# A transformer block in fp32: which engine subtracts the softmax maximum beside the feed-forward layers

## The chip, the core and the metric

The kernel runs on one core of one Trainium2 chip. A core has five engines with instruction queues of their own: TensorE (PE in the profile; its weight loads are listed as PEld), VectorE (DVE), ScalarE (ACT), GpSimd (POOL), and SyncE (SP), which here only issues transfers. Each engine works through its queue in order. The metric is the device time of one execution in microseconds (us). Before the change three runs gave 3252.26, 3256.43 and 3268.8 us; their median, 3256.43 us, is the time before.

## The reference

One pre-norm transformer block on x of shape (2, 1024, 1024): attention with 32 heads of size 32 over 1024 tokens, then a gated feed-forward layer of width 2752, all in fp32.

```python
def attn(x, qkvw, qkvb, ow, ob):
    qkv = x @ qkvw + qkvb                     # 1024 -> 3 * 1024
    ...
    scores = jnp.einsum('bhqd,bhkd->bhqk', q, k) * scale
    probs = jax.nn.softmax(scores, axis=-1)
    ctx = jnp.einsum('bhqk,bhkd->bhqd', probs, v)
    ...
    return ctx @ ow + ob

def ffn(x, W_gate, W_up, W_down):
    up = xt @ W_up.T
    gate = jax.nn.silu(xt @ W_gate.T)
    return (gate * up @ W_down.T).reshape(out_shape)

x = x + attn(_layernorm(x), ...)
x = x + ffn(_layernorm(x), ...)
```

## The kernel before

**Phases and units.** Attention is cut into four phases (two batches, two blocks of 512 queries each), and each phase into 16 units of two heads. A unit works through eight key tiles `kt` of 128 keys. For each tile it holds scores of 128 keys by 1024 (two heads by 512 queries), keys on the partitions. Unit `n` belongs to phase `n // 16`.

**What a unit does** (class `Unit`):

- `scores` (matmul L510) writes two score tiles into PSUM (tag `s`, two buffers). `largest` (L524, VectorE) folds each into a running maximum `top`, reading the scores from PSUM; `keep` (L529, ScalarE) copies them to `p` in SBUF. Both have to be done before the PSUM buffer is free for the next scores.
- `maximum` takes the maximum over keys on VectorE (L549, L550, L567, L568), stores its negative to DRAM (L573) and loads it again, broadcast to all partitions, into `m` (L576).
- `less_maximum` (L580 to L590) adds `m` to `p` in place, 128x1024 elements with both inputs in SBUF (L583). The engine is chosen in L582.
- `exponential` (L593, ScalarE) follows, again in place.
- `add` (L606) adds neighbouring tiles of `p`, three additions for each group of four tiles, a running sum: tile 1 gets tile 0, tile 2 gets tile 1, tile 3 gets tile 2. In phase 0 VectorE does all of them; in phases 1 to 3 tiles 3 and 7 go to VectorE and tiles 1, 2, 5 and 6 to GpSimd. `differences` (L599, GpSimd) prepares the values so that these sums may stand in for the tiles themselves.
- `values` (matmuls L622) multiplies with the values and with ones, into PSUM (tag `acc`, one buffer), and `finish` copies the result out.

**What runs beside it.** While phase 0 runs, TensorE does the projections to q, k and v (L371, L433) for both batches, and GpSimd adds up weights for later (L1189). While phases 1, 2 and 3 run, TensorE does the rest of the block for the 512 tokens of the phase before: the output projection (L785, evicted by VectorE at L797), the second normalization with its transposes (L259), and the feed-forward layer. Beside the tail, the rest for the last 512 tokens, there is no attention.

**The feed-forward layer** uses seven products instead of eight for two-by-two blocks. `product` makes gate and up (matmuls L927): each product of four matmuls goes to one PSUM bank and is evicted by VectorE (L941 to L954) or ScalarE (L939); `silu` (L955) and the product of gate and up (L957, VectorE, both inputs in SBUF) follow. After every four chunks of 128 hidden columns a down projection follows, `down_steps`: `down7` (matmuls L1076), whose accumulators VectorE adds to the residual `x` (L1089, L1091), one or two such operations for two matmuls; `sums_h` forms the sums of hidden columns on VectorE (L1045 to L1051, both inputs in SBUF). `down` (L1003, L1014) is the plain form for the last part, and `hold` and `release` (L1026, L1027 on GpSimd; L1032, L1034 on VectorE) change the residual into the form that the seven products need and back. All these accumulators share three PSUM banks (tag `lin`, `lps`). GpSimd also multiplies the attention output by the reciprocal sums (L733) and adds the output bias to `x` (L777).

**What sets the order.** No scheduler reorders instructions. `Emitter` walks through lists of steps with a virtual clock: `run` interleaves the paced attention steps (one beat for each key tile) with the steps of the filling work, and `later(delay, fn)` puts off a step until the virtual clock has passed the delay. The order in which steps come out is the order in each engine's queue, and the tile framework adds the waits. `less_maximum` is a step of its own in `attention_steps`, eleven beats after the scores of the same tile; it puts off the exponential by 3.5 us of the virtual clock and the addition by 8.1 to 10 us. The choice of an engine does not enter the virtual clock.

Of the kernel before, what the change touches and what calls it, by code (L numbers as in the profile page):

```python
# [130 lines left out]
def preln_block_kernel(  # L131
# [14 lines left out]
    nc = tc.nc  # L146
# [318 lines left out]
    class Unit:  # L465
# [113 lines left out]

        def less_maximum(self, kt):  # L580
            p = self.p[kt]
            eng = nc.vector if self.phase == 0 and kt % 4 == 3 else nc.gpsimd  # L582
            eng.tensor_tensor(p, p, self.m, ALU.add)  # L583
            em.later(3500.0, lambda: self.exponential(kt))
            if kt % SUMS > 0:

                vec = self.phase == 0 or kt % RUN == RUN - 1
                delay = 8100.0 if self.phase == 0 else 10000.0 if vec else 9500.0
                eng = nc.vector if vec else nc.gpsimd
                em.later(delay, lambda: self.add(kt, eng))  # L590
# [767 lines left out]
```

## Time and profile before

| what | before |
|---|---|
| median of three runs | 3256.43 us |
| the profiled execution, its span | 3272.8 us |
| mean granted TensorE clock | 0.986 |
| L583 on GpSimd | 480 instructions, 1197.0 us, mean 2.508 us |
| L583 on VectorE | 32 instructions, all between 165.1 and 788.2 us |
| L606 on GpSimd | 192 instructions, 466.8 us, mean 2.431 us |
| L606 on VectorE | 192 instructions, 328.1 us, mean 1.709 us |
| L524 on VectorE (top from top) | 384 instructions, 469.1 us, mean 1.222 us |
| L1089 on VectorE | 360 instructions, 235.7 us, mean 0.680 us |
| ScalarE's wait at L593 for GpSimd's L583 | 325.6 us |
| GpSimd's wait at L606 for ScalarE's L593 | 346.8 us |

The profile is of one execution, so sums of its durations are to be compared with its own span. The span runs from the first to the last instruction. A group's line gives its busy time, the mean duration of one instruction, and the idle time of its engine just before it with what ended that. A line of the timeline gives start, duration, engine, source line and operation, then in brackets the idle time before it and what ended it; `x3` means that three neighbours were merged. Phase 0 takes the first 890 us or so, phases 1 to 3 lie between 890 and 2790 us, and the tail follows. A wait counted for an engine costs time only where the engine is the one that the end waits for.

### The profile page before, as it was taken

Reading aid. Unit: us, or ns where it says so; the run is one execution under the profiler, and the core shown is the slowest. Engines: PE = TensorE matmul, PEld = TensorE weight load, DVE = VectorE, ACT = ScalarE, POOL = GpSimd, SP = SyncE. Lnnn points to the kernel's source line nnn. Section 1 sums busy time; section 2 is a strip of 40 time slices with the busy share of each in tenths; the row PEclk is TensorE's granted clock in tenths of the full one; section 3 lists DMA queues with packets and bytes.
Section 4 is the critical chain, followed back from the end, with each engine's and each line's share of the span. In section 5 each row is a group of like instructions: output and inputs, shape, how many; then the busy total and the mean of one; then the engine's idle time right before and its main releaser. Section 6 shows DMA issues by size and latency. Waiting matters only on the chain.

```text
span 3272.8 us, 42759 instructions
## 1 busy us (share of the span) xinstructions
PE 3166.3 (97%) x15488; PEld 1785.6 (55%) x15488; DVE 2012.2 (61%) x2733; ACT 1446.8 (44%) x1585; POOL 2039.6 (62%) x1079
## 2 busy tenths in 40 slices
PE   8999999999999999998899999988999999999999
PEld 4444434444346666563376655633756567477775
DVE  2266766776356777766577777666777774344334
ACT  2244554544456555563665555635655554010000
POOL 0267766777788777667887777777877777200000
PEclk9999999999999999998999999989999999999999
DMA  4566756655434554555344444562445445544452
GB/s 154 167 182 203 228 181 197 195 186 164 145 109 139 155 150 150 149 153 180 98 146 150 148 146 146 151 184 92 140 146 151 149 140 149 168 152 154 153 153 96
DMA packets 337825, 507.24 MB, mean 155 GB/s; under 512 B 105424, under 2 KB 122064, under 8 KB 337616
## 3 DMA queue, kind: packets, MB, share of 16 engines
q1 hardware_dynamic: 281424, 405.91, 40.4%
q10 hardware_dynamic: 56192, 98.60, 9.8%
q8 instruction: 124, 2.03, 0.3%
q14 instruction: 85, 0.70, 0.1%
HBM read 429.14 MB, written 75.24 MB: 154 GB/s over the span
## 4 chain that ended last, share of the span: by engine, by line
PE 79%; DVE 8%; POOL 4%; DMA 3%; issue 3%; ACT 2%; SPq 1%; ACTq 0%; POOLq 0%; DVEq 0%
PE p L927 30%; PE pq L371 13%; PE pd L1076 9%; PE acc L622 8%; PE s L510 7%; PE pvv L433 6%; PE po L785 4%; POOL p L583 2%; DVE x L1089 2%; DVE top L524 1%; DVE p L606 1%; PE pd L1003 1%; PE pg L971 1%; POOL p L606 1%; DVE h L957 1%
## 5 line engine op out<-in xcount | busy, mean ns | idle before, releaser
L583 POOL TENSOR_TENSOR p<-p,m 128x1024 f32<-128x1024 f32 x480 | 1197.0, 2508 | 15.9 <-DMA m<-d 15.9
L529 ACT COPY p<-s 128x1024 f32<-128x1024 f32 x512 | 516.3, 1012 | 730.0 <-DVE top L524 553.6
L593 ACT ACTIVATE p<-p 128x1024 f32<-128x1024 f32 x512 | 529.6, 1056 | 379.2 <-POOL p L583 325.6
L606 POOL TENSOR_TENSOR p<-p,p 128x1024 f32<-128x1024 f32 x192 | 466.8, 2431 | 352.5 <-ACT p L593 346.8
L524 DVE TENSOR_TENSOR top<-s,top 128x1024 f32<-128x1024 f32 x384 | 469.1, 1222 | 289.0 <-PE s L510 272.0
L927 PE MATMUL p<-sum,m 128*128 128x256 f32 x2688 | 610.4, 382 | 1.4 <-ACT gate L939 0.9
L927 PEld LDWEIGHTS p<-sum,m 128*128 128x128 f32 x2688 | 505.2, 190 | 101.1 <-issue 29.3
L927 PE MATMUL p<-xn2T,m 128*128 128x256 f32 x2016 | 469.5, 384 | 0.3 <-ACT xn2T L267 0.2
L371 PE MATMUL pq<-xnT,wqk 128*128 128x512 f32 x1024 | 457.4, 599 | 0.0
L1076 PE MATMUL pd<-wp,h 128*128 128x512 f32 x960 | 432.6, 598 | 15.2 <-DVE x L1089 15.0
L927 PEld LDWEIGHTS p<-xn2T,m 128*128 128x128 f32 x2016 | 382.6, 192 | 87.0 <-issue 29.8
L606 DVE TENSOR_TENSOR p<-p,p 128x1024 f32<-128x1024 f32 x192 | 328.1, 1709 | 105.2 <-ACT p L593 70.4
L371 PEld LDWEIGHTS pq<-xnT,wqk 128*128 128x128 f32 x1024 | 190.2, 190 | 249.4 <-issue 247.7
L510 PE MATMUL s<-q,k 32*128 32x512 f32 x2048 | 312.6, 650 | 12.0 <-ACT p L529 12.0
L1076 PEld LDWEIGHTS pd<-wp,h 128*128 128x128 f32 x960 | 177.7, 190 | 251.1 <-issue 197.0
L1189 POOL TENSOR_TENSOR ws<-raw 128x512 f32<-128x512 f32 x62 | 89.8, 1448 | 298.3 <-DMA raw<-in_w_gu 190.7
L1089 DVE TENSOR_TENSOR x<-pd,x 128x512 f32<-128x512 f32 x360 | 235.7, 680 | 52.6 <-PE pd L1076 52.2
L622 PE MATMUL acc<-p,vals 128*32 128x256 f32 x4096 | 254.6, 389 | 11.3 <-DVE p L606 11.3
L433 PE MATMUL pvv<-wv,xnT 128*128 128x512 f32 x512 | 231.1, 601 | 0.2 <-DVE vv L445 0.2
L785 PE MATMUL po<-wo,ctx 128*128 128x512 f32 x512 | 229.7, 601 | 0.8 <-DMA wo<-in_w_o 0.8
L622 PEld LDWEIGHTS acc<-p,vals 128*32 128x32 f32 x4096 | 121.4, 111 | 181.6 <-issue 97.7
L990 POOL MEMSET h<- 64x512 f32 x4 | 2.1, 524 | 298.9 <-PE pd L1076 298.9
(94 smaller groups left out, 2520.2 us busy)
## 6 DMA issues: line engine op xcount, KB each, us to landing
m<-dws SPq DMA_DIRECT2D x336, 256.0 KB
m<-in_w_gu SPq DMA_DIRECT2D x252, 256.0 KB
wp<-ddn SPq DMA_DIRECT2D x160, 256.0 KB
m<-d SPq DMA_DIRECT2D x64, 512.0 KB
wp<-in_w_dn SPq DMA_DIRECT2D x120, 256.0 KB
raw<-in_w_gu ACTq DMA_DIRECT2D x84, 256.0 KB
dws<-ws ACTq DMA_DIRECT2D x84, 256.0 KB
x<-in_x SPq DMA_DIRECT2D x32, 512.0 KB
```

The lines of the kernel that those rows point to most:

```text
L371: nc.tensor.matmul(ps, wqk[b, g, w, hk][:, k, :], xnT[b, s][:, kc, :], start=(kc == 0), stop=(kc == KC - 1),)
L433: nc.tensor.matmul(st["ps"], xnT[b, t // TB][:, kc, (t % TB) * P : (t % TB + 1) * P], st["w"][kc], start=(kc == 0), stop=(kc == KC - 1),)
L510: nc.tensor.matmul(ps[a][:, h * NH : (h + 1) * NH], self.k[rows, i * P : (i + 1) * P], self.q[rows, :], start=True, stop=True,)
L524: nc.vector.tensor_tensor(self.top, s, self.p[0] if kt == 1 else self.top, ALU.max)
L529: nc.scalar.copy(self.p[kt], s)
L583: eng.tensor_tensor(p, p, self.m, ALU.add)
L593: nc.scalar.activation(self.p[kt], self.p[kt], AF.Exp, scale=SCALE)
L606: eng.tensor_tensor(self.p[kt], self.p[kt], self.p[kt - 1], ALU.add)
L622: nc.tensor.matmul(self.acc[j * HD : (j + 1) * HD, c : c + NQ], w(h), self.p[kt][:, q0 : q0 + NQ], start=start, stop=stop, skip_group_chec ...
L785: nc.tensor.matmul(st["ps"], ctxT[b, blk][:, g, t * P : (t + 1) * P], st["w"][hf, g], start=(g == 0), stop=(g == G - 1),)
L927: nc.tensor.matmul(ps, mats[c, n][:, kc, :], rhs, start=(kc == 0), stop=(kc == hk - 1),)
L1076: nc.tensor.matmul(st["pd"], lefts[n](pi)[:, j, t * P : (t + 1) * P], st["wp", pi, n, j], start=(j == 0), stop=(j == PART // 2 - 1),)
```

## The change

One line in `less_maximum`. In phase 0 the choice stays as it was: tiles 3 and 7 of each unit on VectorE, the others on GpSimd. In phases 1 to 3, beside the output projections and the feed-forward layers, GpSimd did all eight; after the change VectorE does tiles 1, 3, 5 and 7. The operands, the place of the step in the emitted order and the delays of what follows stay the same.

```diff
         def less_maximum(self, kt):
             p = self.p[kt]
-            eng = nc.vector if self.phase == 0 and kt % 4 == 3 else nc.gpsimd
+            mine = kt % 4 == 3 if self.phase == 0 else kt % 2 == 1
+            eng = nc.vector if mine else nc.gpsimd
             eng.tensor_tensor(p, p, self.m, ALU.add)
             em.later(3500.0, lambda: self.exponential(kt))
             if kt % SUMS > 0:
```

## The prediction

> **What bounds the kernel now.** I read the page's totals first, then the chain that ended last, then the stages.
>
> ```profile
> span 3272.8 us, 42759 instructions
> ...
> PE 3166.3 (97%) x15488; PEld 1785.6 (55%) x15488; DVE 2012.2 (61%) x2733; ACT 1446.8 (44%) x1585; POOL 2039.6 (62%) x1079
> ...
> PE 79%; DVE 8%; POOL 4%; DMA 3%; issue 3%; ACT 2%; SPq 1%; ACTq 0%; POOLq 0%; DVEq 0%
> ```
>
> TensorE is the bound: only 107 us of the span are without a matmul. The totals of VectorE (61%) and GpSimd (62%) look alike, but they are averages. So I cut the span into stages with the view of busy time by stretch. Its columns are the stretch, its length, then PE, PEld, DVE, ACT and POOL busy us (instructions), granted clock, DMA share, GB/s. The first line is all that the change touches; the next three are two of the fourteen stretches in which a down projection (L1076) runs beside attention, and the sum of all fourteen.
>
> ```profile
> 890.00:2790.00 1900.00, 1823.10 (x10077) 1093.12 (x10076) 1301.49 (x1816) 1026.53 (x1096) 1471.30 (x746) 0.98 0.48 145
> ...
> 1164.00:1197.00 33.00, 31.29 (x126) 13.19 (x125) 30.45 (x40) 15.22 (x16) 23.19 (x11) 1.00 0.47 140
> ...
> 2376.00:2410.00 34.00, 32.39 (x128) 13.41 (x127) 32.10 (x41) 15.11 (x16) 23.71 (x10) 1.00 0.43 132
> ...
> sum 468.00, PE 449.90 PEld 187.15 DVE 421.67 ACT 213.44 POOL 328.78; mean PE 32.14 PEld 13.37 DVE 30.12 ACT 15.25 POOL 23.48
> ```
>
> In 890 to 2790 us, 77 us are without a matmul. In the fourteen stretches VectorE is busy 421.7 of 468 us (90%), GpSimd 70%: VectorE is nearly full there, not GpSimd. The timeline shows both kinds of stall, one of each below.
>
> ```profile
> 1186.47 2.54 DVE L524 TENSOR_TENSOR top<-s,top 128x1024 f32<-128x1024 f32 x2
> 1188.92 1.28 DVE L1089 TENSOR_TENSOR x<-pd,x 128x512 f32<-128x512 f32 x2
> ...
> 1190.26 1.98 PE L1076 MATMUL pd<-wp,h 128*128 128x512 f32 x4 [1.71 <-DVE x L1089]
> ...
> 1515.78 2.34 POOL L583 TENSOR_TENSOR p<-p,m 128x1024 f32<-128x1024 f32 x1
> 1518.07 2.35 POOL L606 TENSOR_TENSOR p<-p,p 128x1024 f32<-128x1024 f32 x1
> ...
> 1520.45 3.35 DVE L606 TENSOR_TENSOR p<-p,p 128x1024 f32<-128x1024 f32 x1 [8.89 <-POOL p L606]
> ...
> 1523.72 1.87 DVE L1014 TENSOR_TENSOR x<-pd,x 128x512 f32<-128x512 f32 x3
> ...
> 1524.46 1.22 PE L1003 MATMUL pd<-wd,h 128*128 128x512 f32 x1 [8.48 <-DVE x L1014]
> ```
>
> First kind: two maxima stand ahead of the accumulator's eviction in VectorE's queue, and TensorE waits 1.71 us for a PSUM bank. Second kind: VectorE waits 8.89 us for GpSimd's addition, TensorE 8.48 us behind it. I went through every TensorE gap over 0.25 us between 890 and 2790 us: eleven go back to GpSimd (1.25, 0.28, 3.20, 8.48, 0.48, 0.38, 2.69, 1.66, 11.70, 1.31, 8.44: 40 us), all where one block's down projection or output projection hands over to the next; some 18 us are short waits for VectorE in the down projections; four, together 15.6 us, stand ahead of the transposes of the second normalization.
>
> **What a subtraction costs on VectorE.** The change removes 192 instructions from GpSimd (4 of 8 key tiles, 16 units, 3 phases) and puts 192 into VectorE's queue; the instruction lists of both programs show just this, and no other step, DMA or queue entry moves. GpSimd loses 192 x 2.46 us (its mean at L583 from 890 us on) = 472 us. What VectorE pays depends on what GpSimd does meanwhile:
>
> ```profile
> 0.00:890.00 890.00, 60.23 (x32) 300.09 (x113) 0.99 0.58 182
> ...
> 1177.47 1.21 DVE L606 TENSOR_TENSOR p<-p,p 128x1024 f32<-128x1024 f32 x1
> ...
> 2239.51 12.18 DVE L606 TENSOR_TENSOR p<-p,p 128x1024 f32<-128x1024 f32 x1
> ```
>
> The first line is L583 alone in the first stage, where VectorE already does a quarter of the subtractions: 60.23 / 32 = 1.88 us each. The second is an operation of the same shape with GpSimd idle: 1.21 us. The 3.35 us above and the 12.18 us here began while GpSimd ran. Of the 92 VectorE additions from 890 us on, the 55 that met no GpSimd instruction took 1.21 us on average, the 31 that began during one 2.68 us. The maxima at L524 (one input from PSUM) take 1.22 us either way. So with both inputs in SBUF a VectorE operation is held while GpSimd works. Bounds per subtraction: 1.21 and 2.68 us. I take 1.88: the same line, and GpSimd's share there (548 of 890 us, 62%) is near what it falls to (below).
>
> The Trainium skill, "SBUF — State Buffer", section "Who interferes with whom", speaks against this change: a VectorE instruction with two SBUF inputs contends with a GpSimd instruction that reads SBUF, and the one that issues second is blocked until the first finishes. The 3.35 us agrees, but the 12.18 us does not: five GpSimd tensor operations passed during it. By the rule a single loss is at most 2.36 + 1.21 us, and 192 such would be 685 us of VectorE time; by the row there is no such cap.
>
> **The sum by stage.** *Down projections.* 86 subtractions start on GpSimd in the fourteen stretches; half, 43, move: 43 x 1.88 = 81 us. Against that, the four feed-forward sums of each stretch (L1045 to L1051, means 1.41, 1.17, 1.49 and 1.70 us against 0.68 alone) lose 3.06 us per stretch to GpSimd, 43 us in all; GpSimd's time there falls by 43 x 2.46 = 106 of 329 us, a third, so 14 us come back. VectorE then needs 421.7 + 81 - 14 = 489 us. The fullest stretch now reaches 97% (31.06 of 32 us); of 468 us that is 454. What does not fit, 35 us, falls on TensorE, because the moved operation stands straight behind the maxima and ahead of the next eviction, as in the first stall; what is late next is the matmul that needs the bank. Bounds: at 1.21 us with all 43 us returned nothing is pushed out and TensorE's 18 idle us could go: -18; at 2.68 us and nothing returned, 421.7 + 115 - 454 = 83.
>
> *The rest.* The other 141 moved operations (367 / 2 - 43) add 265 us to 880 of 1432 us: VectorE goes from 61% to 80%. In the gate and up products the cover is two further PSUM banks, each four matmuls of 0.215 us, 1.7 us together: 1.21 hides, 2.68 is 1.0 over. Without that cover, a third held of some 100 such operations costs 33 us. A pair of maxima (2.55 us) passes there without a stall now, so I take 5. The four transposes stand behind VectorE steps: one operation each, 4 x 1.88 = 7. Together 12, bounds 0 and 40.
>
> *Gain.* In the 8.48 and 11.70 us stalls one of the subtractions ahead of GpSimd's addition goes: 2 x 2.34; in the 2.69 us one the same, 2.3. The 8.44 us stall is the 12.18 us operation, held by an unbroken GpSimd run with L583 three times in it; with a hole in that run it goes: 8.4. The 1.66 and 3.20 us stalls I leave: VectorE is full there too. That is 15.4 us. The granted clock in these places is 0.81, 0.77 and 0.87 (1485 to 1530, 2160 to 2190, 2230 to 2270 us): 31.9 x 0.19 + 18.3 x 0.23 + 31.6 x 0.13 = 14 us, of which 15.4 / 28.6, some 7, come back. Gain 22; bounds 0 and 40 + 14 = 54. A second wait for the broadcast maximum costs nothing: GpSimd's even tile waits for the same transfer one beat earlier.
>
> Sum: 35 + 12 - 22 = +25 us on the profiled 3272.8, that is 3298. The profiled execution lies 16 us (0.5%) over the runs' median of 3256.43, so the forecast for the median is **3281 us**.
>
> **Rivals.** *GpSimd's relief decides (faster).* For it: all long stalls go back to GpSimd, which is 77% busy from 890 us on (1471 of 1900) and would fall to 54%. Against it: VectorE is fuller in the down projections. If most operations fall into the holes that they make, at 1.21 us: 43 x 1.21 - 14 = 38 against 32 us of room, +6, nothing elsewhere, and all 40 us of stalls gone: -34, 3222 us. It decides from a mean price below 1.30 us, where 43p - 14 - 32 + 12 equals 22.
> *Hidden anyway.* Small stalls on both sides cancel; for it: TensorE's queue keeps its order and 97%. 3256 us.
> *Starvation (slower still).* One of 92 additions was held for 12.18 us and stopped TensorE for 8.44 us at a clock of 0.87 (4 us more). At that rate 192 operations bring two: +25, 3306 us. Against it: GpSimd's runs get shorter. It matters from two events on.
> *That it doesn't do what it says* is out by the instruction lists.
>
> **How the numbers follow.** Forecast (slower, by VectorE in the down projections) 0.48, starvation 0.07, relief 0.27, hidden 0.18. A measurement of this kernel can tell about 0.5%, 16 us, from no change. So slower 0.55, within 0.18, faster 0.27. All bounds together give -72 to +123 us (3184 to 3379); eight in ten I put between 3220 and 3335, which holds the relief's 3222 and starvation's 3306. The likeliest case's own range is 3262 to 3312.
>
> **What would show it.** After: VectorE near 2350 us busy and GpSimd near 1570; L583 on VectorE 224 times at about 1.9 us; the fourteen stretches longer by 2 to 3 us each, with VectorE at 95% and more, and L1076 waiting for L1089 some 50 us instead of 18; the handover stalls of 8 to 12 us shorter, with a higher clock. I am wrong if the down projections keep their length (relief), or if gate and up products begin to wait for VectorE by tens of us (then it is slower than I say).

## The result and the profile after

The change makes the kernel slightly slower: 3275.68 us (median of 13 runs, 3269.82 to 3280.12) against 3257.06 us (13 runs, 3252.26 to 3275.14), a ratio of 1.004 with a 95% interval of 1.0027 to 1.0054. A second measurement gave 1.0031 (1.0015 to 1.0046). The ratios stand for +13 and +10 us (the medians of the two measurements lie 19 and 9 us apart). The forecast was 3281 us; its direction held, and its size, +25 us, is about twice what the ratios show.

The page of the profiled execution after: span, engine totals, and the chain that ended last.

```profile
span 3270.6 us, 42718 instructions
...
PE 3161.7 (97%) x15488; PEld 1777.3 (54%) x15488; DVE 2242.6 (69%) x2925; ACT 1447.0 (44%) x1585; POOL 1655.0 (51%) x887
...
PE 73%; DVE 18%; ACT 3%; DMA 3%; issue 2%; POOL 1%; SPq 0%; ACTq 0%; DVEq 0%; POOLq 0%
```

GpSimd's share of the chain falls from 4% to 1%, VectorE's rises from 8% to 18%. The bound has not moved from TensorE (97%); what TensorE waits for has. The groups of the changed line, L584 now, on both engines (busy us, mean ns):

```profile
L584 POOL TENSOR_TENSOR p<-p,m 128x1024 f32<-128x1024 f32 x288 | 750.5, 2611 | 20.6 <-DMA m<-d 20.5
...
L584 DVE TENSOR_TENSOR p<-p,m 128x1024 f32<-128x1024 f32 x224 | 404.1, 1804 | 0.0
```

192 subtractions moved, at 1.79 us each from 890 us on. VectorE's total rose by 230 us, though its subtractions rose by 344 (404.1 - 60.2). Some 84 us came off operations that GpSimd had held before: 32 us at the product of gate and up (from 1.51 to 1.00 us each for the 63 from 890 to 2790 us), 29 at the additions (328.1 to 299.1), 15 at the feed-forward sums and 8 at the operations on the residual with two SBUF inputs. The rest, some 29 us, is mostly that neighbouring instructions overlap a little in the record, so that their durations add up to more than the engine's busy time. GpSimd's own subtractions got longer, from 2.46 to 2.62 us: the hold goes both ways.

The timeline at the two places whose lines from before stand in the prediction. First a down projection:

```profile
1180.87 2.54 DVE L524 TENSOR_TENSOR top<-s,top 128x1024 f32<-128x1024 f32 x2
...
1183.33 1.22 DVE L584 TENSOR_TENSOR p<-p,m 128x1024 f32<-128x1024 f32 x1
...
1184.46 1.28 DVE L1090 TENSOR_TENSOR x<-pd,x 128x512 f32<-128x512 f32 x2
...
1185.79 1.98 PE L1077 MATMUL pd<-wp,h 128*128 128x512 f32 x4 [2.55 <-DVE x L1090]
```

The subtraction stands between the maxima and the eviction, and TensorE's wait has grown from 1.71 to 2.55 us. Then the handover from one block to the next:

```profile
1498.09 1.92 DVE L584 TENSOR_TENSOR p<-p,m 128x1024 f32<-128x1024 f32 x1
...
1510.85 2.34 POOL L584 TENSOR_TENSOR p<-p,m 128x1024 f32<-128x1024 f32 x1
...
1513.15 2.35 POOL L607 TENSOR_TENSOR p<-p,p 128x1024 f32<-128x1024 f32 x1
...
1515.53 3.36 DVE L607 TENSOR_TENSOR p<-p,p 128x1024 f32<-128x1024 f32 x1 [4.35 <-POOL p L607]
...
1519.54 2.08 PE L1004 MATMUL pd<-wd,h 128*128 128x512 f32 x2 [6.33 <-DVE x L1015]
```

Before, GpSimd did one more subtraction here, that of tile 7 of the unit, ahead of the lines that stand in the prediction:

```profile
1511.99 2.35 POOL L583 TENSOR_TENSOR p<-p,m 128x1024 f32<-128x1024 f32 x1
```

Now VectorE does that one, at 1498.09, so one subtraction (at 1510.85) instead of two stands directly ahead of GpSimd's addition, and TensorE's wait fell from 8.48 to 6.33 us. Waits of TensorE for VectorE from 890 to 2790 us (us in total, times, longest), first before, then after:

```profile
PE pd L1003 <- DVE x L1014: 20.2, 2, 11.7
PE pd L1076 <- DVE x L1089: 17.9, 26, 1.7
...
PE acc L622 <- DVE p L606: 11.3, 3, 8.4
```
```profile
PE pd L1077 <- DVE x L1090: 36.0, 39, 3.4
PE pd L1004 <- DVE x L1015: 16.1, 3, 9.5
...
PE acc L623 <- DVE p L607: 1.0, 1, 1.0
```

To see where the time went, I took lengths from each trace, from TensorE's own instructions: the four *handovers* (the first from the first output projection matmul, the others from a block's last matmul of L1076, each to the first gate product), the fourteen *down projections* beside attention (each from its first to its last matmul of L1076), and the *products*, the fifteen stretches that lead up to a down projection.

| profiled execution | handovers, each and sum, us | 14 down projections, us | products, us |
|---|---|---|---|
| before | 82.9, 121.2, 130.4, 75.3: 409.8 | 458.7 | 1081.0 |
| before, again | 83.3, 124.1, 127.9, 75.4: 410.7 | 458.1 | 1079.8 |
| before, a third time | 83.3, 127.1, 121.4, 72.4: 404.2 | 458.2 | 1080.0 |
| after | 76.7, 111.8, 115.4, 72.1: 376.0 | 483.3 | 1089.0 |
| after, again | 81.2, 113.4, 115.6, 72.2: 382.4 | 482.8 | 1088.2 |

On average: down projections +24.7 us, products +8.3, handovers -29. Of the last, 19 us are waits of TensorE (its idle time in the handovers fell from 45 to 26 us), and 10 us are shorter matmuls; the granted clock there rose from 0.94 to 0.97 on average. By place the sum is +4; the ratios say +10 to +13. Part of the difference may be chance in which executions were profiled: the three spans of before, 3266 to 3273 us, lie at or above the medians of before, 3257 to 3266 us. It was not followed further.

### The profile page after: what moved, and what is told of

Read it like the earlier page. It is cut to its first block, busy times and chain, and to the rows that moved or that the text cites. A ratio compares the mean times of both kernels' runs of the same rounds, so it can differ in the third digit from the quotient of the medians.

```text
span 3270.6 us, 42718 instructions
## 1 busy us (share of the span) xinstructions
PE 3161.7 (97%) x15488; PEld 1777.3 (54%) x15488; DVE 2242.6 (69%) x2925; ACT 1447.0 (44%) x1585; POOL 1655.0 (51%) x887
## 4 chain that ended last, share of the span: by engine, by line
PE 73%; DVE 18%; ACT 3%; DMA 3%; issue 2%; POOL 1%; SPq 0%; ACTq 0%; DVEq 0%; POOLq 0%
PE p L928 28%; PE pq L371 13%; PE s L510 7%; PE pd L1077 6%; PE acc L623 6%; PE pvv L433 6%; PE po L786 5%; DVE top L524 4%; DVE p L584 3%; DVE x L1090 3%; DVE p L607 1%; PE pd L1004 1%; DVE part L550 1%; ACT p L529 1%; PE pg L972 1%
## 5 line engine op out<-in xcount | busy, mean ns | idle before, releaser
L607 POOL TENSOR_TENSOR p<-p,p 128x1024 f32<-128x1024 f32 x192 | 498.3, 2595 | 693.5 <-ACT p L594 684.6
L584 POOL TENSOR_TENSOR p<-p,m 128x1024 f32<-128x1024 f32 x288 | 750.5, 2611 | 20.6 <-DMA m<-d 20.5
L1077 PE MATMUL pd<-wp,h 128*128 128x512 f32 x960 | 438.5, 602 | 32.8 <-DVE x L1090 32.3
L584 DVE TENSOR_TENSOR p<-p,m 128x1024 f32<-128x1024 f32 x224 | 404.1, 1804 | 0.0
L607 DVE TENSOR_TENSOR p<-p,p 128x1024 f32<-128x1024 f32 x192 | 299.1, 1558 | 91.4 <-ACT p L594 67.1
L1077 PEld LDWEIGHTS pd<-wp,h 128*128 128x128 f32 x960 | 176.3, 190 | 275.3 <-issue 187.8
L510 PE MATMUL s<-q,k 32*128 32x512 f32 x2048 | 304.6, 646 | 7.9 <-ACT p L529 7.9
L623 PE MATMUL acc<-p,vals 128*32 128x256 f32 x4096 | 254.7, 390 | 1.2 <-DVE p L607 1.0
L1190 POOL TENSOR_TENSOR ws<-raw 128x512 f32<-128x512 f32 x62 | 99.5, 1605 | 306.7 <-DMA raw<-in_w_gu 186.9
L623 PEld LDWEIGHTS acc<-p,vals 128*32 128x32 f32 x4096 | 121.5, 111 | 170.1 <-issue 96.3
```

The source lines that it names most:

```text
L510: nc.tensor.matmul(ps[a][:, h * NH : (h + 1) * NH], self.k[rows, i * P : (i + 1) * P], self.q[rows, :], start=True, stop=True,)
L607: eng.tensor_tensor(self.p[kt], self.p[kt], self.p[kt - 1], ALU.add)
L623: nc.tensor.matmul(self.acc[j * HD : (j + 1) * HD, c : c + NQ], w(h), self.p[kt][:, q0 : q0 + NQ], start=start, stop=stop, skip_group_chec ...
L1077: nc.tensor.matmul(st["pd"], lefts[n](pi)[:, j, t * P : (t + 1) * P], st["wp", pi, n, j], start=(j == 0), stop=(j == PART // 2 - 1),)
```

## Experiments

Ratios are to runs of the kernel before on the same chip, with 95% intervals.

**The kernel before, twice more** (no edit).

> The kernel before, profiled once more. If the 12.18 us addition and the handover stalls belong to the kernel, they come again at the same places and the span is near 3273 us; if they are chance, this span is some 10 us shorter and they sit elsewhere.

> The same a third time, for the spread of the handovers between executions of one kernel: the same lengths within 1 us if they are fixed, 5 us and more apart if they depend on how the engines happen to fall against each other.

Spans 3271.9 and 3266.3 us. The down projections repeat within 0.6 us, the handovers do not (the third: 130.4, 127.9, 121.4). What differs is the long hold of VectorE. The group of L606 on VectorE (minimum, median, maximum in ns), the second profile:

```profile
L606 DVE TENSOR_TENSOR p<-p,p x92: 1202/1216/12183, 903.5 to 2773.8; 128x1024 f32<-128x1024 f32 x92
```

and the timeline of the third:

```profile
1584.78 9.88 DVE L606 TENSOR_TENSOR p<-p,p 128x1024 f32<-128x1024 f32 x1
```
```profile
1583.86 4.71 POOL L583 TENSOR_TENSOR p<-p,m 128x1024 f32<-128x1024 f32 x2
1588.49 2.38 POOL L606 TENSOR_TENSOR p<-p,p 128x1024 f32<-128x1024 f32 x1
1590.79 2.37 POOL L583 TENSOR_TENSOR p<-p,m 128x1024 f32<-128x1024 f32 x1
1593.09 2.42 POOL L599 TENSOR_TENSOR vals<-vals 128x128 f32<-128x128 f32 x3
```

Each of the three profiles has a hold of 10 to 12 us, in a varying handover (one has two, 9.89 and 12.18), always in an unbroken GpSimd run. Neither profile after has one over 3.42 us. So the lost time there comes with this kernel each time, and its place varies.

**Only in the handovers, and only in the down projections.** The emitter carries the name of the place whose matmuls were emitted last; the choice asks for it (for the second kernel, for "down").

```diff
+        self.place = "handover"          # Emitter
...
         def product(c, n, kc):
+            em.place = "products"
...
         def down7(pi, n, t, j):
+            em.place = "down"
...
         def down(pi, hf, t, ci):         # and project() of oproj_steps
+            em.place = "handover"
...
-            mine = kt % 4 == 3 if self.phase == 0 else kt % 2 == 1
+            mine = kt % 4 == 3 if self.phase == 0 else kt % 2 == 1 and em.place == "handover"
```

> The odd tiles go to VectorE only between the last down projection of a block and its successor's first gate product (40 of the 192 moves). Theory (relief at the handovers, price in the down projections): 15 to 30 us faster than before, 3227 to 3242 us, with the down projections at their old length. Rival (the handover stalls have another cause, or come back behind the next wait): within 8 us of before.

> The odd tiles go to VectorE only while the seven-product down projections are emitted (42 of the 192 moves). Theory: VectorE is over its capacity there, so 15 to 35 us slower than before, 3272 to 3292 us, and L1076 waits 15 us or more longer for VectorE. Rival (VectorE pays in the gate and up products, or the price hides): 0 to 5 us slower.

Handovers alone: 3248.81 against 3266.17 us, ratio 0.9949 (0.993 to 0.9968). The handovers fall to 389.8 us in sum, the down projections stay at 458.3. This beats both kernels. Down projections alone: 3281.22 us, ratio 1.0046 (1.003 to 1.0061), with 22.6 us more in the down projections (480.8) and none in the products (1080.2). Its handovers sum to 398.7 us, some 10 below before, though nothing moved there; one of them still has a hold of 9.88 us. TensorE's waits there, handovers alone and down projections alone:

```profile
PE pd L1082 <- DVE x L1095: 17.5, 24, 1.8
```
```profile
PE pd L1082 <- DVE x L1095: 33.6, 36, 3.2
```

17.5 us is the old value, 33.6 nearly that of the whole change (36.0). Both theories of place held, at the lower ends of what I expected, and the 42 moves in the down projections alone cost some 15 us, about what all 192 together lose.

**The relief by itself.** GpSimd's odd subtractions go and VectorE gets nothing: these tiles keep their maximum, so the result is not the block's.

```diff
-            eng.tensor_tensor(p, p, self.m, ALU.add)
+            if self.phase == 0 or kt % 2 == 0:
+                eng.tensor_tensor(p, p, self.m, ALU.add)
```

> The subtraction of tiles 1, 3, 5 and 7 is left out in phases 1 to 3, so GpSimd is relieved and VectorE gets nothing. Theory: the handovers alone gain, 20 to 40 us faster than before, 3217 to 3237 us. Rival (GpSimd's time is hidden anyway): within 8 us of before.

3223.4 us, ratio 0.9867 (0.9843 to 0.989): 43 us faster, a little more than expected. Handovers 381.8 (-26), down projections 444.8 (-13.5), products 1076.8 (-3.5). I had expected the handovers alone to gain; the down projections gain too. The relief is worth 43 us, and some 53 to 56 us (43 + 10 to 13, each difference by its ratio) is what VectorE's part of the change costs.

**VectorE's work by itself, free of GpSimd.** A reduction of the broadcast maximum (one SBUF input) at the exact places of the moved subtractions; in the second kernel GpSimd is relieved as above.

```diff
             eng.tensor_tensor(p, p, self.m, ALU.add)
+            if self.phase > 0 and kt % 2 == 1:
+                nc.vector.tensor_reduce(
+                    idle, self.m.rearrange("p (b j) -> p b j", j=HD), AX.X, ALU.max
+                )
```

> GpSimd keeps all its subtractions; at the places where the change puts its 192 subtractions VectorE gets a reduction of the broadcast maximum instead, about 1.2 us with a single SBUF input. Theory (VectorE's working time costs, held or not): 25 to 45 us slower than before. Rival (the time held by GpSimd costs): 0 to 8 us slower.

> The subtraction of tiles 1, 3, 5 and 7 is left out in phases 1 to 3, and VectorE gets the same reduction of about 1.2 us in its place: the change with a third of its price gone and nothing to be held by. Theory: the relief of 43 us less some 35 us of work, 0 to 20 us faster than before. Rival: nearly as fast as the relief alone, 30 to 45 us faster than before.

The reduction's group in the first of them (minimum, median, maximum in ns):

```profile
L586 DVE TENSOR_REDUCE idle<-m x192: 1195/1208/1220, 795.3 to 2780.6; 128x32 f32<-128x1024 f32 x192
```

None of the 192 was held, beside a GpSimd at 62%. With GpSimd unrelieved the work costs 30 us, as the theory had it: 3296.16 against 3266.45 us, 1.0091 (1.0059 to 1.0123); down projections 483.3, products 1088.2. With GpSimd relieved it is 3241.95 us, 0.9928 (0.9901 to 0.9955): 19 us of the relief's 43 are used up (handovers 375.6, down projections 467.0, products 1080.8). That is between the theory's 0 to 20 us faster and the rival's 30 to 45. So both seem to count: with GpSimd relieved, 1.21 us of work for each moved subtraction (231 us in all) costs 19 us, and the step from there to the change, which adds 111 us on VectorE (1.21 to 1.79 us each), costs another 34 to 37 us (ratios 0.9928 against 1.0031 to 1.004). The intervals of the two relieved kernels reach 8 to 9 us to either side. By place the two steps are 20 us (1903.4 to 1923.4 in sum) and 27.5 us (to 1950.9, the mean of the two profiles after). For each us of VectorE that is some 0.08 us for the work and 0.25 to 0.33 for the rest.

That the rest is the hold is a reading and not shown by itself: the subtraction, unlike the reduction, also holds GpSimd up (2.62 us for each of GpSimd's own subtractions, 2.42 with relief and work) and releases the exponential. TensorE's waits speak for VectorE's queue rather than for the exponential. L1076's wait for the eviction, first in the relief alone, then with relief and work:

```profile
PE pd L1077 <- DVE x L1090: 7.3, 14, 1.3
```
```profile
PE pd L1082 <- DVE x L1095: 23.2, 27, 2.5
```

After the change it is 36.0 us, while the matmuls on the exponentials (L623) wait 1.0 us in all.

**VectorE's work straight behind the maximum.** The running maximum of the odd tiles is taken twice.

```diff
                     nc.vector.tensor_tensor(self.top, s, self.p[0] if kt == 1 else self.top, ALU.max)
+                    if self.phase > 0 and kt % 2 == 1:
+                        nc.vector.tensor_tensor(self.top, s, self.top, ALU.max)
```

> GpSimd keeps all its subtractions; VectorE repeats the running maximum of tiles 1, 3, 5 and 7 in phases 1 to 3, 192 operations of 1.22 us with one input in PSUM, at nearly the place of the moved subtraction. Theory (VectorE's plain working time is what costs): 43 of them in the down projections need 52 us where 32 are free, so 15 to 30 us slower than before, 3272 to 3287 us. Rival (the loss comes from being held by GpSimd): 0 to 6 us slower.

3329.82 us, ratio 1.0197 (1.0171 to 1.0222): 64 us slower, twice what I expected. The down projections grow to 508.2 us: 50 us for the 42 repeats that start there, 51.4 us of work, so nearly all of it shows up in TensorE's time. The products grow by 20 us (1100.4), the handovers shrink by 15 (393.2). The waits of TensorE, first here, then with the reductions, as many and as long:

```profile
PE pd L1078 <- DVE x L1091: 56.5, 49, 3.2
```
```profile
PE pd L1081 <- DVE x L1094: 34.1, 39, 3.1
```

Work of equal length at another place in VectorE's queue costs twice as much. Here it stands straight behind the maxima and reads the score buffer in PSUM, whose release it puts off; which of the two costs more was not separated.

**Work in the handovers without relief, and everywhere but in the down projections.** The first adds the reduction only where `em.place` is the handover, and GpSimd keeps everything; the second moves the subtraction where `em.place != "down"`.

> As the kernel before, with the reduction of about 1.2 us on VectorE added in the handovers alone, GpSimd keeping all its subtractions. If the gain of moving only there comes from GpSimd's relief: 0 to 10 us slower than before. Rival (any displacement of the two queues against each other loosens the handover): 8 to 20 us faster.

> The odd tiles go to VectorE everywhere but in the seven-product down projections (150 of the 192 moves). Theory: the handover's gain less some 8 us for the gate and up products, 5 to 20 us faster than before, a little slower than moving in the handovers alone. Rival (VectorE pays in the products too as soon as it is over 80% there): as slow as the change, 10 us slower than before.

The first: 3262.03 against 3265.68 us, 0.999 (0.9977 to 1.0003), outside both expectations. Its handovers sum to 395.1 us, 13 below before, and no addition was held longer than 3.36 us. The other three kernels that leave GpSimd its subtractions in the handovers show the same, 10 to 15 us less (398.7, 395.7, 393.2). So nearly half of the 29 us that the profiles show for the change comes without relief there. The time of this one shows little of it: 3 us by the ratio, whose interval includes 1. The relief is what separates it from the 0.9949 of the handovers alone: 13 us. The second: 3264.63 us, 0.9998 (0.9985 to 1.0011), where I expected 5 to 20 us faster. Handovers 385.1, but products 1088.2 (+8) and down projections 466.7 (+8, though nothing moved there). VectorE's delay in the products is carried into the next down projection: VectorE is busy 428.2 us there instead of 418.1, without one moved subtraction. Against moving in the handovers alone (0.9949), the 110 moves in the products so cost some 16 us (the two intervals leave 7 us to either side), as much as the 42 in the down projections.

**Handovers and the down projection before each.**

```diff
         def down7(pi, n, t, j):
+            em.place = "handover" if pi == WHOLE - 1 else "down"
```

> As moving in the handovers alone, and also in each block's last seven-product down projection, just before the handover (46 moves). If GpSimd's backlog from there sets the handover: 5 to 10 us faster than moving in the handovers alone. Rival (VectorE is full there too): the last down projections 2 to 4 us longer each and no gain.

3247.64 us, 0.9944 (0.9927 to 0.9961): the same as the handovers alone. The handovers shrink to 377.5 us, as in the whole change, and the down projections grow to 464.2: 12 us won, 6 paid, by the profiles; the times can't tell the two kernels apart.

## Why the prediction was right, and where its sizes were off

- *Direction and mechanism: shown in the main.* VectorE in the down projections pays (down projections alone: 1.0046), and the handovers give part of it back (handovers alone: 0.9949). A price that I had nearly left out is as large: that of the moves in the products (below).
- *"1.88 us" per subtraction:* measured 1.79 on average, 1.21 where no GpSimd instruction ran and 2.18 when one was running at the start; 1.68 in the down projections.
- *"35 us" in the down projections:* measured 24.7, and two errors cancel in part. VectorE's busy time there grew by 40.5 us (418.1 to 458.6), where I had 67 (81 - 14): the 42 subtractions that start there took 70.6 us, the four sums gave 15.5 us back (83.5 to 68.0; I had 14), and other held operations got shorter too, which I had not counted. But of the 40.5 us only 16 found room, where I had 32: VectorE ended at 95% (458.6 of 483.3 us), not at 97%.
- *"12 us" for the rest:* 8.3 in the products, where the transposes fall too. I had put 7 on the transposes and 5 on the gate and up products. The transposes' waits grew by 2.6 us (16.0 to 18.6), those of the gate and up products by 3.5 (1.6 to 5.1), so they did not begin to wait by tens of us. What I missed is that VectorE's delay is handed on: the products' moves cost some 16 us when they are made without those in the down projections, half of it in the next down projections.
- *"22 us" gained at the handovers:* 29 by place: 19 of waits, where I had 15.4, and 10 of shorter matmuls at a higher clock, where I had 7. Some 13 of it, by the profiles, comes without relief as well, and not all of it by the steps named. The 8.48 and 11.70 us stalls fell by 2.15 and 2.25 us (to 6.33 and 9.45), close to the 2.34 that I took off each. The 12.18 us hold did go, but it was absent from that handover in the third profile of before and in the kernels with work and no relief, so that its going is due to relief is not shown. This term, 8.4 us, was a matter of chance.
- *The sum, +25 us:* +10 to +13 by the ratios. This is below the 0.5% that I named as the limit of telling, to which I had given 0.18; the two intervals put it above zero all the same. That 3281 us lies within 6 us of the measured 3275.68 is partly luck: errors of both signs in the terms, and medians that lie further apart here than the ratio says.
- *Relief decides:* not for this change. Below the 1.30 us at which I let it decide, with unheld work of 1.21 us and GpSimd relieved, the kernel is 24 us faster than before, where I had 34.
- *Starvation:* not seen after; the long holds were in the kernel before.
- *What I said would be seen:* L1077's wait for VectorE 36 us instead of some 50; the down projections 1.8 us longer each instead of 2 to 3; VectorE at 2243 us instead of 2350; GpSimd at 1655 us instead of 1570, because its own instructions are held as well (1561 us in the relief alone, whose profile has the same GpSimd instructions); the clock from 1485 to 1530, 2160 to 2190 and 2230 to 2270 us from 0.81, 0.77 and 0.87 to 0.92, 0.83 and 1.00.

## What to carry to other kernels

Before moving work between two engines, cut the trace by stage: the 42 moves in the down projections cost 15 us, the 110 in the products some 16, the 40 in the handovers gain 17, and the totals of the engines (61% and 62%) told none of it. Price a VectorE operation with two SBUF inputs by what GpSimd does meanwhile, and try more than one place in the queue for new work: 192 operations of 1.2 us cost 30 us at one place and 64 at another.

## What the runs showed of the hardware

A VectorE operation with both inputs in SBUF can be passed over by several GpSimd instructions in a row: 9.88 us behind an unbroken run, 12.18 us in another, for work of 1.21 us. The Trainium skill, "SBUF — State Buffer", section "Who interferes with whom", has the later one blocked until the first finishes; the usual holds here (up to 3.42 us after the change, one GpSimd instruction of 2.36 us and the work itself) fit that, the long ones do not. A reduction with one SBUF input was never held (192 times, 1.195 to 1.220 us), as that section says.
